# Starting the first pair's scans after the sources of its first image

## The chip, the cores and the metric

The kernel runs on one core of one Trainium2 chip. The metric is device time in microseconds (us); the figure of a kernel is the median of its runs. Five engines work side by side, each with its own queue of instructions in a fixed order: PE (TensorE, matmuls; PEld is its weight loading), DVE (VectorE), ACT (ScalarE), POOL (GpSimd) and SP (SyncE, which here only starts transfers). ACT starts transfers too.

## The reference, cut to what matters

Input and output are 8 images of 64 channels and 64 x 64 pixels, in fp32. Four layers follow each other: an attention over all 4096 pixels with small convolutions (layer 0), two blocks of windowed attention with an MLP (layer 1), a dynamic 3 x 3 filter with a 1 x 9 convolution (layer 2), and a state space layer (layer 3). Only layer 3 concerns the change:

```python
xz = jnp.einsum('bhwc,dc->bhwd', x, in_proj_w) + in_proj_b
xi, z = jnp.split(xz, 2, axis=-1)
xc = jax.nn.silu(_dwconv3(jnp.transpose(xi, (0, 3, 1, 2)), conv_w, conv_b))   # sources of the scans
x_hwwh = [xc, xc transposed over the pixels], each also run backwards          # 4 directions
# per direction k and pixel t, for 128 channels x 16 states:
h = h * jnp.exp(dt_t[..., None] * A) + dt_t[..., None] * B_t[:, :, None, :] * u_t[..., None]
y_t = jnp.einsum('bkcn,bkn->bkc', h, C_t)
y = _ln(y, outnorm_g, outnorm_b) * jax.nn.silu(z)                              # then a last projection
```

Each image has its own scan. What the scan of an image reads (`xc` and its transpose) and what its result is later multiplied with (`silu(z)`) depend on that image alone. This is what the document calls the sources of an image.

## The kernel before, in words

**Pairs of images.** Two images of 64 channels fill the 128 partitions, so the 8 images are 4 pairs. For a pair `p`, `front(p)` (a Python generator) does layers 0 to 2 and then `scan_sources(p)`; `scans(p)` does the scans; `back(p)` does the rest of layer 3.

**The sources.** `scan_sources` first normalises the whole pair into `H3`, 8 chunks of 512 pixels, and stores `X` to memory as `x2`. Then, for each of the two images in turn: 8 matmuls into the bank `pi` (L1610) that ACT copies into a padded picture `XI` (L1613); a 3 x 3 convolution by nine DVE operations for each chunk, the first on L1256 and eight on L1252; a Silu on ACT into `xcv` (L1620), a transposed copy into `XT` (L1621) and a store to `xc` (L1622); four stores of `XT` to `xt` (L1625); and 8 matmuls for `z` with a Silu (L1639) and a store to `zs` (L1640). All these stores are started from ACT's queue. Silu and Exp need different tables on ACT, so a change between them puts an `ACT_TABLE_LOAD` ahead of the operation.

**The scans.** The 2 images x 4 directions x 8 blocks of 512 pixels are 64 units, each of 8 steps, so a pair has 512 steps. A step handles two states: SP fetches rows of B and C, spread to all partitions (L1720); POOL multiplies B by the input (`products`, L1725); ACT makes two exponentials (`dad`, L1747); DVE runs two scans (L1750); ACT keeps the last values (`carry`, L1758); POOL or DVE multiply by C (L1761 and L1765); PE adds the products up (L1789). Once per unit `inputs` loads a block of sources (`xs`, L1697) and makes `du` and the rows of B and C from it. The tiles of B and C have three buffers.

**Work beside the scans.** `scans` takes a generator `beside` with its estimated `cost`. Every `yield` gives a cost in made-up units; after each step the generator is advanced until the work done matches the share of steps done, `cost * (i + 1) / (n - LEAD)` with `n` = 512 and `LEAD` = 24. So the work is spread evenly over 488 steps. Beside the scans of pair 0 runs `front(1)` from layer 1 on; beside pair 1 `back(0)` and `front(2)`; beside pair 2 `back(1)` and `front(3)`; beside pair 3 `back(2)`. The final order on each engine is made by a scheduler that starts from this program order.

**The head.** `begin` runs `front(0)` to its end, with layer 0 of pair 1 beside it (`_Apart.first`, with a pace of its own set by `AHEAD`), and only then opens the buffers of the scans. So before the first scan of image 0 the sources of images 0 and 1 are both made. `front` and `first`, the summed costs of a whole front and of its layer 0, are measured here and set the pace of all later pairs.

Of the kernel before, what the change touches and what calls it, by code (L numbers as in the profile page):

```python
# [19 lines left out]
NCH = L // CH  # L20
WS, NH, HD = 8, 8, 8
SHIFT = 4
TAPS = 9
# [212 lines left out]
class _Net:  # L236
    def __init__(self, ctx, tc, x, packs, layout, out):
        self.tc, self.nc = tc, tc.nc
        self.x, self.out = x, out
        nc = self.nc  # L240
        self.const = ctx.enter_context(tc.tile_pool(name="const", bufs=1))
        self.dram = ctx.enter_context(tc.tile_pool(name="rows", bufs=2, space=bass.MemoryType.DRAM))
        self.packs, self.layout, self.w = packs, layout, {}
        self.load(self.const, (0, 1))
        with tc.tile_pool(name="temp", bufs=1) as temp:
            self.load(temp, (2,))
            self.prepare()
# [410 lines left out]
    def window_attention(self, i, T, pools):  # L658
# [4 lines left out]

        H0, H = self.flat("H0"), self.flat("H")
        H03 = H0.rearrange("p (h w) -> p h w", w=64)
        H5 = H.rearrange("p (y x r c) -> p y x r c", y=8, x=8, c=8)

# [19 lines left out]
        for wy in range(8):  # L687
            cols = slice(wy * CH, (wy + 1) * CH)
            rows = H[:, cols]
            pq = ps.tile([P, CH], F32, name="pq", tag="mm")  # L690
# [10 lines left out]
        def scores(wy, wx):  # L701
# [24 lines left out]
            for half in range(2):  # L726
                nc.tensor.matmul(
                    pv[64 * half : 64 * half + 64],
                    lhsT=H[:, cols],
                    rhs=w[f"vw{i}"],  # L730
# [58 lines left out]
    def mlp(self, i, T, pools):  # L789
        nc, w = self.nc, self.w  # L790
        wk, sm, ps = pools
        H = self.flat("H2")
        self.norm(
            ps, wk, T, w["cen64"], w["avg64"], self.eps[:, 0:1], w[f"norm2_g{i}"], self.norm_to(H, w[f"norm2_b{i}"])
        )
# [362 lines left out]
class _Direct:  # L1158
# [8 lines left out]
    def __init__(self, net, ctx):  # L1167
        self.net, self.tc, self.nc, self.w = net, net.tc, net.nc, net.w
        tc = self.tc
        self.dram = ctx.enter_context(tc.tile_pool(name="mem", bufs=2, space=bass.MemoryType.DRAM))  # L1170
        self.slabs = ctx.enter_context(tc.tile_pool(name="slabs", bufs=3))
        self.ps = ctx.enter_context(tc.tile_pool(name="ps_scan", bufs=3, space=PSUM))
        self.pf = ctx.enter_context(tc.tile_pool(name="ps_front", bufs=3, space=PSUM))
        self.kept = {}
        self.turn = -1
        self.dense = 0

    def begin(self, ctx):


        tc = self.tc
        with tc.tile_pool(name="slabs0", bufs=3) as slabs, tc.tile_pool(name="w00", bufs=2) as pool:
            ahead = _Apart(self, slabs, pool).first(1)
            front = first = done = 0
            for cost in self.front(0):
                front += cost
                if cost == 0:
                    first = front
                while first and done < AHEAD * (front - first):
                    done += next(ahead, front)  # L1190
            self.run(ahead)
        one = ctx.enter_context(tc.tile_pool(name="scan1", bufs=1))
        self.Y = one.tile([P, L], F32, name="Y", tag="Y")
        self.carries = one.tile([P, NST], F32, name="carry", tag="carry")
        self.sw = ctx.enter_context(tc.tile_pool(name="scan", bufs=2))
        return front, first

    def work(self, name):
        return self.tc.tile_pool(name=name, bufs=2)
# [392 lines left out]
    def scan_sources(self, p, X2):  # L1592

        nc, tc, w, net, half = self.nc, self.tc, self.w, self.net, self.HALF
        x2 = self.memory("x2")
        with tc.tile_pool(name="w3", bufs=2) as wk:
            H = self.flat("H3")
            for c in range(NCH):
                cols = slice(c * CH, (c + 1) * CH)
                nc.sync.dma_start(x2[:, cols], X2[:, cols])  # L1600
                pc, sd = self.normed(wk, lambda pc: [(pc, X2[:, cols])], w["cen64"], w["avg64"], net.eps[:, 0:1])
                nc.vector.scalar_tensor_tensor(H[:, cols], pc, w["ln1_g"], sd, ALU.mult, ALU.mult)
                nc.scalar.activation(H[:, cols], H[:, cols], AF.Identity, bias=w["ln1_b"])
                yield 6
            for im in range(2):
                xc, xt, zs = self.memory("xc"), self.memory("xt"), self.memory("zs")
                pad = self.padded("XI")
                for c in range(NCH):
                    pi = self.bank("pi")
                    nc.tensor.matmul(  # L1610
                        pi, lhsT=w["inT"][half[im], 0:P], rhs=H[half[im], c * CH : (c + 1) * CH], start=True, stop=True
                    )
                    nc.scalar.activation(self.rows(pad, c), self.img(pi), AF.Identity, bias=w["in_b"][:, 0:1])  # L1613
                    yield 2
                XT = self.flat("XT").rearrange("p (w h) -> p h w", h=64)
                for c in range(NCH):
                    acc = self.bank("xacc", (P, 8, 64))
                    yield from self.dwconv(acc, pad, 8 * c, 8, w["cw"], w["cb"])
                    cv = wk.tile([P, 8, 64], F32, name="xcv", tag="xcv")
                    nc.scalar.activation(cv, acc, AF.Silu)  # L1620
                    last = nc.scalar.activation(XT[:, 8 * c : 8 * c + 8, :], cv, AF.Copy)  # L1621
                    nc.scalar.dma_start(xc[:, c * CH : (c + 1) * CH], cv.rearrange("p a b -> p (a b)"))  # L1622
                    yield 2
                for s in range(4):
                    nc.scalar.dma_start(  # L1625
                        xt[:, 1024 * s : 1024 * s + 1024],
                        XT.rearrange("p h w -> p w h")[:, 16 * s : 16 * s + 16, :].rearrange("p w h -> p (w h)"),
                    )
                for c in range(NCH):
                    pz = self.bank("pz")  # L1630
                    nc.tensor.matmul(
                        pz,
                        lhsT=w["inT"][half[im], P : 2 * P],
                        rhs=H[half[im], c * CH : (c + 1) * CH],
                        start=True,
                        stop=True,
                    )
                    z = wk.tile([P, CH], F32, name="z", tag="z")
                    last = nc.scalar.activation(z, pz, AF.Silu, bias=w["in_b"][:, 1:2])  # L1639
                    nc.scalar.dma_start(zs[:, c * CH : (c + 1) * CH], z)  # L1640
                    yield 2
                net.log_exp(last)
                self.kept[2 * p + im] = (xc, xt, zs)
        self.kept["x", p] = x2


    @staticmethod
# [264 lines left out]
@with_exitstack  # L1912
def tile_kernel(ctx: ExitStack, tc: tile.TileContext, x: bass.AP, packs, layout, out: bass.AP):
    net = _Net(ctx, tc, x, packs, layout, out)
    with ExitStack() as path:
        net.open(path, True)
        d = _Direct(net, path)
        net.log_exp()
        front, first = d.begin(path)
        back = 0.25 * front  # L1920
        for p in range(B // 2):
            works, cost = [], 0
            if p:
                works.append(d.back(p - 1))
                cost += back
            if p + 1 < B // 2:
                works.append(d.front(p + 1))
                cost += front if p else front - first
            d.scans(p, d.chain(*works), cost)
        d.run(d.back(B // 2 - 1))  # L1930

    with tc.tile_pool(name="check", bufs=1) as pool:
        bad = net.in_range(pool)
    with tc.If(bad > 0), ExitStack() as path:
        net.open(path, False)
        for p in range(B // 2):
            t = net.layer0(p)
            t = net.layer1(t)
            t = net.layer2(t)
            net.layer3(t, p)  # L1940
# [21 lines left out]
```

## Time and profile before

| what | value |
| --- | --- |
| median of 3 runs | 13519.48 us (13518.94, 13519.48, 13551.32) |
| the profiled execution | 13549.57 us, span 13547.6 us |
| busy share of the span: PE, DVE, ACT, POOL | 80%, 65%, 52%, 57% |
| first POOL product of pairs 0, 1, 2, 3 at | 2191.2, 4767.4, 7988.3, 11180.4 us |
| last POOL product | 13279.5 us |
| mean granted TensorE clock | 0.882 |

The times in the trace count from the start of the span. A group's row names line, engine, operation and tiles, then its count, busy time, mean and the idle time of the engine before it with what ended that. "Releaser" is whatever a waiting instruction was waiting for. A row of the stretches gives start and end, length, busy time with instruction count for PE, PEld, DVE, ACT and POOL, then granted clock, the mean busy share of the 16 DMA engines, and GB/s.

### The profile page before, as it was taken

The page shows a single profiled execution, that of the slowest core. Times are in us where ns is not written, and L with a number is a line of the kernel's source. Part 1 is how long each engine was busy: PE and PEld are TensorE (multiplying, and loading weights), DVE is VectorE, ACT ScalarE, POOL GpSimd, SP SyncE. Part 2 cuts the span into 40 slices and gives each one's busy share as a digit, 9 for nine tenths or more (in the row PEclk, how much of TensorE's full clock was granted, in tenths as well). Part 3 has the DMA queues.
Part 4 walks back from the last instruction along what each step waited for, and adds up shares of the span by engine and source line. Part 5 has one row for each costly group of instructions (what it writes and reads, how often), then busy time and mean ns, then how long its engine had stood idle before and what let it go on. Part 6 is the DMA issues. An engine that isn't in the chain of part 4 may idle for free. (4 is left out here: it accounts for less than half of the span.)

```text
span 13547.6 us, 140341 instructions
## 1 busy us (share of the span) xinstructions
PE 10802.4 (80%) x45762; PEld 3981.2 (29%) x45762; DVE 8783.4 (65%) x10407; ACT 7087.6 (52%) x15569; POOL 7764.9 (57%) x3875
## 2 busy tenths in 40 slices
PE   9999986888787669989888667997898666666665
PEld 2243322333232222224432222223443222222221
DVE  0121236776668676676666767667675768988985
ACT  5556514564545646655554545665653644544542
POOL 0000004887778764466666685446675687777881
PEclk9999977998898779999889788998888788888887
DMA  0000004776667765455555674455554677787882
GB/s 24 1 1 1 3 13 170 238 238 211 207 218 244 235 200 168 155 186 175 169 178 175 221 250 168 158 167 176 186 192 151 209 241 262 235 280 264 303 283 86
DMA packets 706249, 2385.12 MB, mean 176 GB/s; under 512 B 81120, under 2 KB 81248, under 8 KB 704480
## 3 DMA queue, kind: packets, MB, share of 16 engines
q1 hardware_dynamic: 681312, 2319.76, 50.9%
q10 hardware_dynamic: 24192, 56.29, 1.1%
q8 instruction: 362, 5.93, 0.2%
q14 instruction: 383, 3.14, 0.1%
HBM read 2272.97 MB, written 102.76 MB: 175 GB/s over the span
## 5 line engine op out<-in xcount | busy, mean ns | idle before, releaser
L1725 POOL TENSOR_TENSOR vd<-B,du 128x1024 f32<-128x1024 f32 x2048 | 4832.8, 2367 | 3924.8 <-DMA B<-rows 2573.0
L1789 PE MATMUL yd<-vd,pack 128*128 128x512 f32 x7540 | 4263.8, 696 | 1381.0 <-POOL vd L1761 591.9
L1747 ACT ACTIVATE dad<-du,As 128x512 f32<-128x512 f32 x4096 | 2729.0, 681 | 1130.8 <-DVE hd L1750 684.1
L1750 DVE TENSOR_TENSOR_SCAN hd<-dad,carry,vd 128x512 f32<-128x512 f32 x2166 | 2713.2, 1270 | 677.8 <-ACT dad L1747 385.9
L1789 PEld LDWEIGHTS yd<-vd,pack 128*128 128x128 f32 x7540 | 1497.0, 215 | 3843.5 <-issue 1654.4
L1761 POOL TENSOR_TENSOR vd<-hd,C 128x1024 f32<-128x1024 f32 x658 | 1551.4, 2358 | 1068.2 <-DVE hd L1750 702.0
L1750 DVE TENSOR_TENSOR_SCAN dad<-dad,carry,vd 128x512 f32<-128x512 f32 x1418 | 1793.3, 1274 | 160.3 <-POOL vd L1725 99.1
L1765 POOL TENSOR_TENSOR vd<-hd,C 128x512 f32<-128x512 f32 x1154 | 1476.1, 1280 | 512.5 <-DVE hd L1750 446.4
L1313 ACT ACTIVATE e<-s 128x512 f32<-128x512 f32 x2048 | 1200.7, 591 | 751.1 <-PE s L1307 749.6
L1307 PE MATMUL s<-X 64*128 64x512 f32 x4096 | 1344.4, 646 | 30.5 <-ACT e L1313 28.8
L1299 PE MATMUL po<-e,VT 128*64 128x512 f32 x4096 | 1226.7, 621 | 12.6 <-ACT e L1313 9.9
L1765 DVE TENSOR_TENSOR vd<-dad,C 128x512 f32<-128x512 f32 x1300 | 864.9, 672 | 48.2 <-ACT carry L1758 39.1
L1758 ACT ACTIVATE carry<-hd 128x1 f32<-128x1 f32 (+1 forms) x1586 | 317.3, 201 | 920.3 <-DVE hd L1750 917.0
L1758 ACT ACTIVATE carry<-dad 128x1 f32<-128x1 f32 x1422 | 240.9, 169 | 804.1 <-DVE dad L1750 801.4
L1307 PEld LDWEIGHTS s<-X 64*128 64x128 f32 x4096 | 375.9, 186 | 915.2 <-issue 783.1
L1447 DVE TENSOR_TENSOR w_e<-w_s,bias 128x512 f32<-128x512 f32 x512 | 329.9, 681 | 424.3 <-PE w_s L1435 423.6
L1462 PEld LDWEIGHTS w_av<-vals,w_e 64*64 64x64 f32 x16384 | 546.7, 144 | 197.3 <-issue 86.8
L1462 PE MATMUL w_av<-vals,w_e 64*64 64x9 f32 x16384 | 574.9, 207 | 30.4 <-ACT w_e L1452 30.1
L1700 PE MATMUL pdd<-xs,xdt 128*128 128x512 f32 x512 | 348.3, 768 | 257.8 <-DMA xs<-xc 121.4
L1452 ACT ACTIVATE w_e<-w_e 128x512 f32<-128x512 f32 x512 | 311.8, 626 | 366.9 <-DVE w_e L1447 251.6
L1299 PEld LDWEIGHTS po<-e,VT 128*64 128x64 f32 x4096 | 236.1, 135 | 847.5 <-issue 763.9
L1574 PE MATMUL acc<-tap,pack 128*128 128x512 f32 x576 | 367.5, 761 | 99.5 <-DVE tap L1573 98.1
(252 smaller groups left out, 11129.2 us busy)
## 6 DMA issues: line engine op xcount, KB each, us to landing
B<-rows SPq DMA_DIRECT2D x2048, 512.0 KB, 5.2
C<-rows SPq DMA_DIRECT2D x2048, 512.0 KB, 4.6
xs<-xt SPq DMA_DIRECT2D x128, 256.0 KB, 3.5
xs<-xc SPq DMA_DIRECT2D x128, 256.0 KB, 4.2
xc<-xcv ACTq DMA_DIRECT2D x64, 256.0 KB, 4.0
zs<-z ACTq DMA_DIRECT2D x64, 256.0 KB, 3.7
xt<-XT ACTq DMA_DIRECT2D x32, 512.0 KB, 7.8
rows<-bc SPq DMA_DIRECT2D x256, 64.0 KB, 1.6
```

The lines of the kernel that those rows point to most:

```text
L1299: nc.tensor.matmul(po[half[im]], lhsT=VT[:, t, half[im]], rhs=es[im], start=(t == 0), stop=(t == 31))
L1307: nc.tensor.matmul(ss[im], lhsT=at(half[im], t), rhs=X[half[im], jc * CH : (jc + 1) * CH], start=True, stop=True)
L1313: nc.scalar.activation(e, ss[im], AF.Exp, scale=C**-0.5, accum_out=parts[:, im, t, jc : jc + 1])
L1462: nc.tensor.matmul(self.av[half[im], x % 4 + j, h, :], lhsT=es[h // 4][half[im], j, h % 4, :], rhs=V[half[im], x + j, h, :], start=True, s ...
L1574: nc.tensor.matmul(acc, lhsT=w["ident"], rhs=tap, start=(t == 0), stop=(t == TAPS - 1))
L1725: self.nc.gpsimd.tensor_tensor(v, st["B"], dx.to_broadcast([P, 2, TD]), ALU.mult)
L1747: nc.scalar.activation(da, u["du"][:, 0], AF.Exp, scale=net.As[:, k, n : n + 1])
L1750: nc.vector.tensor_tensor_scan(along(to), along(da), along(v[:, j]), first, ALU.mult, ALU.add)
L1758: nc.scalar.activation(cs, ends, AF.Copy)
L1761: st["w"] = nc.gpsimd.tensor_tensor(v, h, CC, ALU.mult)
L1765: m = engine.tensor_tensor(v[:, j], hs[j], CC[:, j], ALU.mult)
L1789: m = nc.tensor.matmul(u["y"], lhsT=w["ident"], rhs=v, start=start, stop=stop)
```

## The change

The scans of pair 0 begin once the sources of image 0 exist. `scan_sources` ends each image with `self.ready = 2 * p + im` and a `yield 0`; `begin` stops reading the generator when `ready` is 0, opens the scans' buffers and hands the unfinished generator back. Beside the scans of pair 0 that rest (the sources of image 1) runs first, then `front(1)` as before. Its cost is set to `more` = 8 x (0.7 x 9 + 6) = 98.4 units, which is added to the cost beside pair 0 and to `front`, so that `front` has the same value as before. `H3` is allocated outside the work buffers, and the chunk buffers of each image (`w3i`) are opened and closed for each image, so that none is open while `begin` opens others. The arithmetic is the same.

```diff
@@ class _Direct: __init__, begin
+        self.ready = -1
...
-            for cost in self.front(0):
+            works = self.front(0)
+            for cost in works:
                 front += cost
-                if cost == 0:
+                if cost == 0 and not first:
                     first = front
+                if self.ready == 0:
+                    break
                 while first and done < AHEAD * (front - first):
                     done += next(ahead, front)
             self.run(ahead)
...
-        return front, first
+        return works, front, first
@@ scan_sources
+        H = self.flat("H3")
         with tc.tile_pool(name="w3", bufs=2) as wk:
-            H = self.flat("H3")
...
-            for im in range(2):
+        self.kept["x", p] = x2
+        for im in range(2):
+            with tc.tile_pool(name="w3i", bufs=2) as wk:
                 xc, xt, zs = self.memory("xc"), self.memory("xt"), self.memory("zs")
...
                 self.kept[2 * p + im] = (xc, xt, zs)
-        self.kept["x", p] = x2
+            self.ready = 2 * p + im
+            yield 0
@@ tile_kernel
-        front, first = d.begin(path)
+        rest, front, first = d.begin(path)
+
+        more = NCH * (0.7 * TAPS + 6)
+        front += more
         back = 0.25 * front
         for p in range(B // 2):
-            works, cost = [], 0
+            works, cost = [rest], more
             if p:
+                works, cost = [], 0
                 works.append(d.back(p - 1))
                 cost += back
```

## The prediction

> **What bounds the kernel now.** I read the page first. Its chain of work that ended last covers only a few per cent of the span, nearly all in the closing `back(3)`, so it says nothing of the head. The change lives between the end of layer 2 of pair 0 and the end of pair 0's scans (2191 to 4767 us), so I took the timeline around the first scan (start, duration, engine, operation, and in brackets the idle time before it):
>
> ```profile
> 2098.09 1.70 ACTq L1640 DMA_DIRECT2D zs<-z  x2
> ...
> 2108.09 0.81 DVE L1256 TENSOR_SCALAR xacc<-XI,pack 128x512 f32<-128x512 f32 x1 [22.06 <-ACT XI L1613]
> ...
> 2110.52 10.62 DVE L1252 SCALAR_TENSOR_TENSOR xacc<-XI,pack,xacc 128x512 f32<-128x512 f32 x16
> ...
> 2173.36 1.76 ACTq L1640 DMA_DIRECT2D zs<-z  x2
> ...
> 2177.62 0.80 SPq L1697 DMA_DIRECT2D xs<-xt  x2
> ...
> 2182.75 0.66 ACT L1702 ACTIVATE pdd<-pdd,pack 128x512 f32<-128x512 f32 x1 [2.19 <-PE pdd L1700]
> ...
> 2191.20 4.67 POOL L1725 TENSOR_TENSOR vd<-B,du 128x1024 f32<-128x1024 f32 x2 [2174.44 <-DMA B<-rows]
> ```
>
> The first `zs` row ends image 0's sources, the second image 1's; between them everything is image 1's. POOL has waited 2174 us for its first product. Next the stretches (columns: PE, PEld, DVE, ACT, POOL busy, clock, DMA share, GB/s):
>
> ```profile
> 2085.00:2165.00 80.00, 35.56 (x39) 10.68 (x38) 49.16 (x77) 27.98 (x37) 0.00 (x0) 0.50 0.28 107
> 2787.00:2935.00 148.00, 115.66 (x286) 40.14 (x290) 100.31 (x104) 102.62 (x189) 128.68 (x64) 0.90 0.67 231
> 3589.00:4165.00 576.00, 479.70 (x1011) 173.63 (x1010) 394.12 (x425) 231.47 (x483) 449.36 (x219) 0.90 0.64 213
> 4249.00:4615.00 366.00, 229.42 (x363) 77.19 (x364) 294.47 (x343) 240.36 (x389) 288.67 (x141) 0.79 0.74 246
> ```
>
> Row one is image 1's sources alone in the head: no engine is full. Row two is scans beside an MLP: POOL 87% busy, DVE 68%. The last is scans beside the sources of pair 1, the very work that is moved: DVE rises to 80%, POOL falls to 79%. The groups on the page give the pace that POOL allows:
>
> ```profile
> L1725 POOL TENSOR_TENSOR vd<-B,du 128x1024 f32<-128x1024 f32 x2048 | 4832.8, 2367 | 3924.8 <-DMA B<-rows 2573.0
> L1761 POOL TENSOR_TENSOR vd<-hd,C 128x1024 f32<-128x1024 f32 x658 | 1551.4, 2358 | 1068.2 <-DVE hd L1750 702.0
> L1765 POOL TENSOR_TENSOR vd<-hd,C 128x512 f32<-128x512 f32 x1154 | 1476.1, 1280 | 512.5 <-DVE hd L1750 446.4
> ```
>
> Two steps of pair 0 take POOL 2 x 2.367 + 2.358 + 1.280 = 8.37 us, or 4.19 us a step. The 512 steps took 2576 us, 5.03 each. So pair 0's scans are paced by POOL's work plus 0.84 us a step of waits.
>
> **What the Trainium skill says.** "Perfetto Trace Analysis", section Optimization Strategy, says that a kernel with several regimes can gain from interleaving them; rows one and two above are such regimes (POOL idle, then 87% busy). "ScalarE: Activation LUTs", section What ACT_TABLE_LOAD costs, gives 1283 ns for a load and about 2.66 us for each change of set with its drain. The trace agrees on the load (1283 ns, in every such row) and shows no separate drain: a load at 4613.11 is followed by its Silu at 4614.40. "DMA: Bandwidth & Descriptors", section Issuing engines are not separate DMA queues, says that transfers started on ACT and SP share 16 engines. That fits the share of 0.74 in the sources row against 0.67 beside the MLP.
>
> **The change part by part.**
>
> *Removed from the head.* Today the first `xs` leaves at 2177.62, 2.5 us after the last `zs` of image 1 was started (2173.36 + 1.76 = 2175.12), since it waits for all earlier stores. After the change it waits for image 0's last `zs`, which ends its start at 2098.09 + 1.70 = 2099.79; so it leaves near 2102.3, 75.3 us earlier. The compiled order puts a table load and six of image 1's `XI` copies ahead of the first `pdd` exponential on ACT. In the trace these run from 2099.81, and the sixth, at 2107.37 plus 0.69, ends at 2108.1. The `xs` landing (some 3 us) and two matmuls end at about 2107.5, so ACT decides: `pdd` at 2108.1 instead of 2182.75, 74.7 us earlier. From there the chain to the first product (8.45 us) is unchanged. Gain: 75 us.
>
> *Moved into the scans.* Image 1's sources: DVE 8 x (0.805 + 8 x 0.745) = 54 us of convolution plus 0.4 of border; ACT 8 x (0.69 + 0.60 + 1.08 + 0.69) = 24 us; PE 16 matmuls of some 0.69 us beside scans, 11 us (0.85 in the head, where the clock is 0.50); 20 stores on ACT's queue. Their pace is 1412.8 units over 488 steps, 2.895 a step, so 98.4 units take 34 steps; `front(1)` then has 454 steps instead of 488 and is 7.5% denser.
>
> *Added.* The compiled orders differ in number by 33 table loads, all on ACT: 33 x 1.283 = 42 us, each between scan exponentials. Every other instruction count is the same, and from the end of pair 0 on the orders agree, so pairs 1 to 3 cost the same. ACT is in order, so behind a load wait the next `dad` exponential and `carry`, then DVE's scan, POOL's product with C, and SP's next fetch, which waits for a buffer of B or C.
>
> *Moved on SP.* The load of pair 1's `X` from `first` (2 MB) is ahead of the first `xs` today; it goes in among B and C fetches near step 30. The compiled order gives it no wait but an earlier transfer, so SP isn't blocked; its bytes are those of two steps' fetches. Unloaded it lands in 8.8 us at most: 0 to 9 us, I take 5.
>
> *What the scans pay.* The trace has the same work beside the same scans: 366 us (last row) hold 72 products, 5.08 us a step, and at 1314.4 / 488 = 2.69 units a step an image takes 36.5 steps, so this is two images. Upper comparison: POOL's floor of 4.19, giving 36.5 x 0.89 = 32 us. Lower: the MLP row, 148 us for 32 steps or 4.62, giving 36.5 x 0.46 = 17 us. The last 48 steps of pairs 1 and 2, with little beside them, take 5.0 to 5.1, so steps without other work don't reach the floor; I take 17. Table loads and stalls on stores are in these steps. If all the denser work must be paid in DVE time, the price is 54 us plus most of the 5; if idle time of DVE and ACT covers it, nothing.
>
> Sum: -75 + 17 + 5 = -53. The profiled execution's 13549.6 us would become 13496.6. The median stands 30.1 us below that execution, and I carry the difference over: 13519.5 - 53 = 13466.5, say 13467, 0.39% faster. About 0.3% (41 us) is what a measurement of this kernel can tell from no change.
>
> **The rivals.**
>
> *All hidden.* POOL and the fetches pace pair 0 whatever stands beside it. For: POOL 87% busy beside light work; in the DVE-heavy stretch it still does 79%. Against: it fell by 8 points there. Time: 13519.5 - 75 = 13444.
>
> *DVE becomes the bound.* Scans need 2 x 1.27 + 0.5 x 0.67 = 2.9 us of DVE a step plus about 0.2 of unit work; 54 us over the 23 steps of the convolution add 2.35, in all 5.4, above POOL's 4.19. Then the moved DVE time is paid nearly in full, 57 us with the 5: 13519.5 - 75 + 57 = 13501, within 0.3%. Against: the same overload in the last row came out at 5.08 over both images, as the scheduler spreads the taps.
>
> *Slower: table changes on ACT's queue.* Image 1 has 16 Silus. If each stops the scan chain for two loads, its own 0.69 and a wait for its staging tile, like
>
> ```profile
> 4629.22 1.28 ACT L1639 ACT_TABLE_LOAD   x1 [4.50 <-DMA zs<-z]
> ...
> 4631.31 1.28 ACT L1747 ACT_TABLE_LOAD   x1
> ```
>
> (the store of `z` is late, and the exponentials stand behind it), that is 2.57 + 0.69 + 4.5 = 7.7 us, times 16 is 124 us: 13519.5 - 75 + 124 = 13568, slower by 0.36%. It decides from 4.7 us a Silu (no gain left), 7.2 us for 0.3%. Against: those two images had 32 Silus and cost at most 65 us above POOL's floor, 2 us each.
>
> *It doesn't do what it says.* The scheduler could pull image 1's work ahead of the scans. The compiled order shows only the six copies and ten convolution taps (7.5 us of DVE, while B is on its way) before the first scan, so this is out.
>
> **How the numbers follow.** Likeliest, 0.52: -53, with its own range 13455 to 13479. All hidden 0.13: 13444 to 13455. DVE bound 0.24: 13480 to 13520. ACT 0.09: above 13560. A rest of 0.02 is spread. Faster by over 0.3%: 0.52 + 0.13 = 0.65; within: 0.26; slower: 0.09. The range from 13440 to 13515 leaves out the ACT case and the edge of the DVE case, with little below.
>
> **What would show it.** Right: the first POOL product near 2116; 33 more table loads; pair 0's scans longer by 10 to 35 us, the length of pairs 1 to 3 unchanged within some 15 us (pairs 1 and 2 differ by 29 today). Wrong: the first product later than 2125 (another wait ahead of `xs`); pair 0 longer by over 50 us, with DVE full in the first 40 steps (DVE rival) or ACT waiting for `zs` and `xc` stores (ACT rival); or pair 0 no longer at all. What would break the sum is the denser `front(1)` costing more than in proportion, seen as steps beside layer 2 above today's 5.2.

## The result and the profile after

| kernel, same runs side by side | median us | lowest to highest |
| --- | --- | --- |
| before | 13530.14 | 13518.94 to 13551.32 (5 runs) |
| changed | 13461.74 | 13452.38 to 13465.75 (5 runs) |

The ratio is 0.995, with a 95% interval of 0.9937 to 0.9963: 0.50% faster. The forecast was faster, 13467 us, range 13440 to 13515. The profiled execution of the changed kernel took 13452.38 us, span 13450.6 (before: 13549.57 and 13547.6).

The code has seven more lines ahead of the scans, so L1697, L1702, L1725, L1747, L1750, L1761 and L1765 of before are L1704, L1709, L1732, L1754, L1757, L1768 and L1772 here. First the timeline around the first scan, in the same columns as before:

```profile
2084.49 1.28 ACT L438 ACT_TABLE_LOAD   x1 [1.20 <-issue]
...
2087.21 0.80 SPq L1704 DMA_DIRECT2D xs<-xt  x2
...
2092.05 0.69 ACT L1619 ACTIVATE XI<-pi,pack 128x512 f32<-128x512 f32 x1 [1.02 <-PE pi L1616]
...
2094.05 0.66 ACT L1709 ACTIVATE pdd<-pdd,pack 128x512 f32<-128x512 f32 x1 [1.32 <-PE pdd L1707]
...
2098.26 5.36 DVE L1256 SCALAR_TENSOR_TENSOR xacc<-XI,pack,xacc 128x512 f32<-128x512 f32 x8
...
2102.42 4.64 POOL L1732 TENSOR_TENSOR vd<-B,du 128x1024 f32<-128x1024 f32 x2 [2085.97 <-DVE xacc L1256]
```

`xs` leaves at 2087.21, `pdd` follows at 2094.05, POOL starts at 2102.42. The convolution taps of image 1 (L1256) already stand beside the first exponentials. From the start of image 0's last `z` store (2083.33 here, 2098.66 in the kernel before) to the first product it is now 19.1 us, and it was 92.5.

The stretches (PE, PEld, DVE, ACT, POOL busy with counts, clock, DMA share, GB/s). First the changed kernel's first 40 steps of scans, now beside image 1's sources; then the first 40 steps of the kernel before, beside layer 1 of pair 1:

```profile
2102.00:2303.00 201.00, 121.44 (x193) 40.19 (x194) 153.99 (x175) 134.64 (x223) 160.47 (x79) 0.79 0.76 256
```

```profile
2191.00:2376.00 185.00, 146.25 (x933) 65.19 (x932) 131.25 (x149) 105.26 (x220) 160.18 (x79) 0.90 0.69 230
```

POOL does the same 160 us of work in both; the 16 us that the changed kernel needs more are POOL standing still. No engine is full: POOL is at 80%, DVE at 77%, ACT at 67%. The clock granted to TensorE is lower here, 0.79 against 0.90. The groups of the changed kernel:

```profile
L1732 POOL TENSOR_TENSOR vd<-B,du 128x1024 f32<-128x1024 f32 x2048 | 4830.1, 2366 | 3847.0 <-DVE xacc L1256 2086.3
L1768 POOL TENSOR_TENSOR vd<-hd,C 128x1024 f32<-128x1024 f32 x658 | 1549.6, 2355 | 1057.4 <-DVE hd L1757 740.8
```

Counts and durations are those of before. What moved is POOL's idle time ahead of the products, 3924.8 to 3847.0.

**Where the time went.** The first products of pairs 0 to 3, the last product and the span's end give lengths. The two single executions compare like this:

| stretch | before | changed | difference |
| --- | --- | --- | --- |
| up to image 0's last `z` store (instructions in the same order) | 2098.7 | 2083.3 | -15.3 |
| from there to the first product | 92.5 | 19.1 | -73.4 |
| pair 0's scans | 2576.2 | 2596.8 | +20.6 |
| pairs 1, 2, 3 | 3220.9, 3192.1, 2099.1 | 3202.9, 3187.7, 2095.5 | -18.0, -4.4, -3.6 |
| after the last product | 268.1 | 265.3 | -2.8 |

The first row isn't the change. Up to there both kernels run the same instructions in the same order; about half of it arose before 113 us and the rest between 680 and 800, in stretches where the granted clock of TensorE differed between the two executions (0.81 against 0.94 between 30 and 60 us, 0.76 against 0.83 between 740 and 780). Two later executions of the changed kernel have their first product at 2124.8 and 2122.9, not 2102.4.

For pair 0 I cut its 512 steps into parts and read each part in every execution, since the same kernel repeats a part better than a whole pair. "Without" are the kernel before and one that leaves image 1's sources out (first experiment); "with" are three executions of the changed kernel:

| steps | without (2) | with (3) | difference of means |
| --- | --- | --- | --- |
| 0 to 40 | 184.7, 185.7 | 200.4, 198.4, 201.8 | +15.0 |
| 40 to 96 | 260.9, 262.9 | 261.5, 257.5, 259.1 | -2.5 |
| 96 to 288 | 951.8, 948.3 | 944.8, 950.6, 935.7 | -6.3 |
| 288 to 416 | 660.1, 656.9 | 653.6, 654.0, 649.8 | -6.0 |
| 416 to 464 | 229.0, 232.4 | 240.9, 241.0, 240.8 | +10.2 |
| 464 to 512 | 289.6, 286.7 | 295.6, 287.8, 288.0 | +2.3 |

So the head gives 73.4 us, and the scans take back 15 where image 1's sources stand and 10 where the sources of pair 1 stand. Both differences are three times the spread within their rows or more. All parts together are +12.6 in the means (2587.1 against 2574.6); that sum is less sure, since pair 0 of the changed kernel alone ranges from 2575.3 to 2596.8. The parts are bounded by step numbers, and image 1's sources stand where layer 1 of pair 1 stood: steps 0 to 40 hold 193 matmuls instead of 931, and steps 96 to 288 hold 5700 instead of 4925. A part therefore shows what a place costs, not what one piece of work costs.

### The profile page after: what moved, and what is told of

Same layout as the page of the kernel before. It is cut to its first block, busy times and chain, and to the rows that moved or that the text cites. A ratio compares the mean times of both kernels' runs of the same rounds, so it can differ in the third digit from the quotient of the medians.

```text
span 13450.6 us, 140381 instructions
## 1 busy us (share of the span) xinstructions
PE 10778.6 (80%) x45762; PEld 3973.8 (30%) x45762; DVE 8785.0 (65%) x10407; ACT 7126.2 (53%) x15602; POOL 7763.5 (58%) x3875
## 5 line engine op out<-in xcount | busy, mean ns | idle before, releaser
L1732 POOL TENSOR_TENSOR vd<-B,du 128x1024 f32<-128x1024 f32 x2048 | 4830.1, 2366 | 3847.0 <-DVE xacc L1256 2086.3
L1796 PE MATMUL yd<-vd,pack 128*128 128x512 f32 x7540 | 4313.5, 703 | 1386.1 <-POOL vd L1768 604.8
L1754 ACT ACTIVATE dad<-du,As 128x512 f32<-128x512 f32 x4096 | 2730.9, 681 | 1115.0 <-DVE hd L1757 669.8
L1757 DVE TENSOR_TENSOR_SCAN hd<-dad,carry,vd 128x512 f32<-128x512 f32 x2166 | 2711.5, 1269 | 679.7 <-ACT dad L1754 406.0
L1768 POOL TENSOR_TENSOR vd<-hd,C 128x1024 f32<-128x1024 f32 x658 | 1549.6, 2355 | 1057.4 <-DVE hd L1757 740.8
L1757 DVE TENSOR_TENSOR_SCAN dad<-dad,carry,vd 128x512 f32<-128x512 f32 x1418 | 1793.0, 1274 | 155.5 <-POOL vd L1732 99.3
L1772 POOL TENSOR_TENSOR vd<-hd,C 128x512 f32<-128x512 f32 x1154 | 1475.7, 1280 | 508.7 <-DVE hd L1757 449.1
L1303 PE MATMUL po<-e,VT 128*64 128x512 f32 x4096 | 1227.9, 622 | 12.6 <-ACT e L1317 9.9
L1772 DVE TENSOR_TENSOR vd<-dad,C 128x512 f32<-128x512 f32 x1300 | 865.3, 672 | 54.1 <-ACT carry L1765 44.9
L1765 ACT ACTIVATE carry<-hd 128x1 f32<-128x1 f32 (+1 forms) x1586 | 316.1, 201 | 901.0 <-DVE hd L1757 898.4
L1765 ACT ACTIVATE carry<-dad 128x1 f32<-128x1 f32 x1422 | 240.8, 169 | 807.8 <-DVE dad L1757 804.7
```

What stands on the lines that cost most here:

```text
L1303: nc.tensor.matmul(po[half[im]], lhsT=VT[:, t, half[im]], rhs=es[im], start=(t == 0), stop=(t == 31))
L1732: self.nc.gpsimd.tensor_tensor(v, st["B"], dx.to_broadcast([P, 2, TD]), ALU.mult)
L1754: nc.scalar.activation(da, u["du"][:, 0], AF.Exp, scale=net.As[:, k, n : n + 1])
L1757: nc.vector.tensor_tensor_scan(along(to), along(da), along(v[:, j]), first, ALU.mult, ALU.add)
L1765: nc.scalar.activation(cs, ends, AF.Copy)
L1768: st["w"] = nc.gpsimd.tensor_tensor(v, h, CC, ALU.mult)
```

## The experiments

Each kernel's times below are beside runs of the kernel before on the same chip. Those medians were 13535.37 us (for the kernels without image 1's sources, with three copies, with one tap and without Silu), 13530.47 (blank units, the changed kernel's second measurement, and the two that move more), 13548.48 (its third, and the first two with spread stores) and 13550.39 (the last). Lengths of pairs and parts come from one execution of each kernel.

### Is the head's gain 75 us, and what does the moved work cost?

Image 1's sources are left out, and its scans read those of image 0. No units are counted for them, so `front(1)` is again spread over 488 steps:

```diff
-            works, cost = [rest], more
+            works, cost = [], 0
+            d.kept[1] = d.kept[0] if p == 0 else d.kept[1]
```

> Left out: the sources of image 1 of the first pair are not made at all; its scans and its last step read those of image 0, so the output for image 1 is another. Everything else is the changed kernel (13462 us, pair 0's scans 2597 us between first products). What this saves against it is the price of the moved work beside the scans; what it saves against the kernel before is the price of the same work in the head. My sum: 17 us beside the scans, so about 13445, pair 0 about 2580; 85 less than before. All hidden: 13462, pair 0 about 2597. DVE bound: 54 us, 13408, pair 0 about 2543.

Measured: 13473.54 us (13453.12 to 13487.89), ratio 0.9955 (0.9941 to 0.9969); pair 0 takes 2572.9 us, the length before; the last `z` store is 17.6 us ahead of the first product. So the head's gain needs nothing but the earlier start. The median alone doesn't show the price of the moved work (it is not even below that of the changed kernel); the parts of pair 0 in the table above do. The waits of the first 40 steps say what the moved work does to the scans (engine, waited for, us in total, times, longest). Without image 1's sources:

```profile
DVE hd L1757 <- ACT dad L1754: 6.9, 3, 4.2
DVE du L1713 <- ACT pdd L1712: 5.7, 3, 2.9
POOL vd L1732 <- DMA B<-rows: 2111.2, 5, 2108.6
```

and in the changed kernel:

```profile
DVE hd L1757 <- ACT dad L1754: 18.7, 8, 4.5
DVE du L1713 <- ACT pdd L1712: 14.1, 2, 11.8
POOL vd L1768 <- DVE hd L1757: 8.9, 6, 3.8
POOL vd L1732 <- DMA B<-rows: 12.0, 6, 5.3
```

DVE now waits for ACT's exponentials 12 us longer, and for `pdd`, where a unit changes, another 8. POOL waits for DVE's scans in turn (0.5 us in the first kernel, where 20.1 us of its waits carry no releaser; 5.7 here). But POOL also waits for rows of B to land: 12.0 us, and 2.6 in the first kernel, where the 2108.6 is the wait ahead of the first product. So the rows show two paths to POOL's 16 us, ACT's queue and late fetches, and don't say how much each is worth.

### Is the price proportional to the work?

Image 1's sources are made three times over (the loop around the whole body, and three times the cost):

```diff
+                for again in range(3 if (p, im) == (0, 1) else 1):
+                    pad = self.padded("XI")
+                    for c in range(NCH):
...
-            works, cost = [rest], more
+            works, cost = [rest], 3 * more
```

> The sources of image 1 of the first pair are made three times over into the same places, and their units are counted three times, so the work beside pair 0 has twice the moved work more. My sum: 2 x 17 = 34 us more than the changed kernel, 13496, pair 0 about 2631. All hidden: 13462. DVE bound: 2 x 54 = 108 more, 13570, pair 0 about 2705. ACT rival (66 more table loads and 32 Silus at 4.7 us and more): 150 or more, above 13610.

Measured: 13622.36 us (13618.27 to 13641.82), ratio 1.0066 (1.0052 to 1.008). Pair 0 takes 2745.3 us, 158 more than the changed kernel's mean: some 79 us for each further copy, where I had priced the first at 17 to 22. Steps 40 to 96 take 335.9 us instead of 259.4 (+76), steps 288 to 416, beside layer 2, 721.0 instead of 652.5 (+68). One place in the first of these, a change of unit on ACT:

```profile
2351.25 1.28 ACT L1710 ACT_TABLE_LOAD   x1
2357.35 2.05 PE L1708 MATMUL pdd<-xs,xdt 128*128 128x512 f32 x2 [5.08 <-DMA xs<-xt]
2359.43 0.66 ACT L1710 ACTIVATE pdd<-pdd,pack 128x512 f32<-128x512 f32 x1 [6.90 <-PE pdd L1708]
2361.18 1.28 ACT L1713 ACT_TABLE_LOAD   x1
2363.56 1.28 ACT L1755 ACT_TABLE_LOAD   x1
2368.18 2.35 POOL L1769 TENSOR_TENSOR vd<-hd,C 128x1024 f32<-128x1024 f32 x1 [13.44 <-DVE hd L1758]
```

`xs` took 7.2 us to land; ACT, in order, stood 6.90 us ahead of `pdd`, then loaded two more tables with unit work between, and POOL stood still for 13.44 us. The further copies bring stalls on stores that the first one doesn't have: the four stores of `XT` of the second and of the third, started in a row, keep ACT's queue for 6.96 us (from 2431.02) and 5.95 us (from 2601.82), and ahead of the borders of the next picture DVE stands 17.05 us, until 2617.62, where a store of `XT` ended last; with one copy it stands 1.84 us at that place. So 79 us is the price of a copy made this way and here, and not of the same work anywhere.

### Does the denser front cost the 68 us?

No sources of image 1, but 295 units of nothing in their place, so that the work of `front(1)` is spread over fewer steps:

```diff
-            works, cost = [rest], more
+            works, cost = [iter([2.0] * 144 + [3 * more - 288.0])], 3 * more
+            d.kept[1] = d.kept[0] if p == 0 else d.kept[1]
```

> Left out: the sources of image 1 of the first pair (its scans read those of image 0). In their place stand 295 units of nothing, as many as the kernel with threefold sources counts, so that about 90 steps run alone and the work for pair 1 is packed into the other 398, 22% denser. If the price beside the scans is proportional to the work, pair 0 stays near 2573 us. If denser work costs more than in proportion, which would be the second part of the 150 us that the threefold sources cost, pair 0 takes about 2630.

Measured: 13485.75 us (13473.31 to 13505.81), ratio 0.9966 (0.9953 to 0.9979); pair 0 2589.7. Steps 288 to 416 take 720.1 us, as with three copies (721.0), and 656.9 without blanks; its layer 2 stands in 76 steps instead of 95. But these steps also hold more: 1722 matmuls instead of 1145, because the MLP ahead of layer 2 now reaches to step 333 instead of 294. Steps 96 to 288, which hold 592 matmuls fewer, take 894.4 instead of 948.3, and the pair is only 17 us longer, not the 57 of my expectation. The first steps were not alone, as I had meant them: the compiled order drew the start of `front(1)` into them (its first score matmul stands at step 13, as without blanks). So the 63 us here, and the 68 with three copies (1835 matmuls in these steps instead of 1178), come with work that has moved across step 288. What the packing of `front(1)` costs is the 17 us of the pair, and these are no larger than the spread of a pair.

### Is it DVE's convolution, or ACT's Silus?

Eight of nine taps of image 1 are left out in one kernel; in the other its Silus are replaced by a copy and by a bias add, so that no table changes:

```diff
+                    if (p, im) == (0, 1):
+                        nc.vector.tensor_scalar(acc, pad[:, 8 * c : 8 * c + 8, 0:64], w["cw"][:, 0:1], w["cb"], ALU.mult, ALU.add)
+                        for t in range(TAPS):
+                            yield 0.7
```

> Left out: eight of the nine taps of the convolution of image 1 of the first pair, so 64 DVE operations (48 us) less beside the scans; pace, Silus, table changes and stores stay. The output of image 1 is another. If DVE time is paid: 48 us less than the changed kernel, 13414. My sum: the scans pay 17 us for all of the moved work, and I put 10 of it on the taps: 13452. All hidden, or the price is ACT's: 13462.

```diff
-                    nc.scalar.activation(cv, acc, AF.Silu)
+                    nc.scalar.activation(cv, acc, AF.Copy if (p, im) == (0, 1) else AF.Silu)
...
-                    last = nc.scalar.activation(z, pz, AF.Silu, bias=w["in_b"][:, 1:2])
+                    last = nc.scalar.activation(z, pz, AF.Identity if (p, im) == (0, 1) else AF.Silu, bias=w["in_b"][:, 1:2])
```

> Left out: the Silu of image 1 of the first pair (a copy, and a sum with the bias, in its place), so that its 16 operations need no change of table and about 33 loads (42 us of ACT) are gone; taps, copies and stores stay. The output of image 1 is another. If the price of the moved work is the table changes: 17 to 20 us less than the changed kernel, 13443. If it is DVE's taps: 13462. My sum: half of 17, 13453.

Measured: one tap 13474.71 us (13439.22 to 13502.7), ratio 0.9954 (0.9937 to 0.9971), pair 0 2587.7; no Silu 13465.79 (13448.53 to 13471.13), ratio 0.9946 (0.9931 to 0.996), pair 0 2578.4. The totals tell nothing apart. The first 40 steps take 196.1 and 195.0 us, against 200.2 with everything and 185.2 with nothing. So leaving out 48 us of DVE work is worth 4 us, and leaving out the Silus' tables (1 load stands in these steps instead of 34) is worth 5; each is one execution, and this part varies by 3.4 us in the changed kernel. Neither is the limit alone: about 10 of the 15 us stay whichever is taken.

The kernel with one tap isn't a clean test of DVE, because its compiled order is another: the stores of `XT` begin at step 14 instead of 28, 22 table loads stand in the first 40 steps instead of 34, and the first 16 steps take 79.2 us instead of 65.1, the next 24 117 instead of 135. A further rival is in both: the clock granted to TensorE in these steps is 0.76 to 0.84 in all kernels with image 1's sources and 0.87 to 0.90 without. No run holds the clock apart.

Without the Silus, DVE's wait for ACT's exponentials is down to 1.3 us, but the one at the change of unit is still there:

```profile
DVE du L1713 <- ACT pdd L1712: 18.2, 2, 15.8
DVE hd L1757 <- ACT dad L1754: 1.3, 2, 1.0
```

### The changed kernel again

> The changed kernel as it is, run beside the next three on one chip. The runs so far leave open whether the moved work costs anything beside the scans: pair 0 took 2597 us with it and 2573 without it in single profiles, but the medians are 13462 with it and 13474 without. If pair 0 shows the price, its length is again 2590 to 2605 us and the median 13460 to 13485. If it is hidden, pair 0 is near 2575.

Measured: 13465.06 us (13430.17 to 13482.99), ratio 0.9947 (0.9933 to 0.9962); first product at 2124.8, pair 0 2589.3. The result holds. A third time, in the last but one set:

> The changed kernel once more, beside the two with spread stores: 13455 to 13470, pair 0's scans 2585 to 2600 us, first 40 steps 197 to 201.

Measured: 13489.64 us (13476.57 to 13510.09) beside 13548.48, ratio 0.9957 (0.994 to 0.9973); first product at 2122.9, pair 0 2575.3, first 40 steps 201.8. Its time and its pair 0 were outside what I had written: a whole pair of one and the same kernel ranges over 21 us, while the first 40 steps stay within 3.4.

### Can more be moved?

In the first kernel image 0's `z` also waits until the scans have begun (16 units more beside them). In the second, image 0's convolution after its first two chunks waits too (66 units more), and image 0's first directions are scanned in the order 0, 1, 3, 2, so that the first units need only these chunks:

```diff
+            if apart:
+                self.ready = 0
+                yield 0
+                with tc.tile_pool(name="w3j", bufs=2) as wk:
+                    yield from zees(wk)
...
+        more = NCH * (0.7 * TAPS + 6) + 2 * NCH
```

> Nothing left out. The eight z of image 0 are made beside the scans too, after the first xs. In the head they hold the last two xcv and the stores of XT back; without them the first product should come 5 to 8 us earlier, against 16 units more beside the scans (3 to 4 us). My theory: 0 to 5 us less than the changed kernel. If the scans hide it all: 8 less.

```diff
+                    yield from conv(wk, range(2, NCH))
+                    yield from zees(wk)
...
+            for nth, k in enumerate((0, 1, 3, 2) if p + im == 0 else (1, 3, 0, 2)):
...
+        more = NCH * (0.7 * TAPS + 6) + 2 * NCH + 6 * (0.7 * TAPS + 2)
```

> Nothing left out. Image 0 begins with the forward direction over rows (order 0, 1, 3, 2 instead of 1, 3, 0, 2), and the scans begin when two of the eight chunks of its convolution are stored; six chunks, the transposed copy and z of image 0 and all of image 1 run beside the scans. The first product should come about 49 us earlier than in the changed kernel; 66 units more beside the scans at 17 to 25 us for 98 units are 11 to 17. Theory of a price in proportion: 32 to 38 us less than the changed kernel, about 13430. If the price grows with the amount, as the threefold sources suggest (74 us for each further 98 units): no gain, 13462 or more.

Measured: 13507.33 us (13456.2 to 13529.83), ratio 0.998 (0.9973 to 0.9987), and 13516.93 (13484.81 to 13544.52), ratio 0.9988 (0.9981 to 0.9995): both slower than the changed kernel. The heads did what was meant: from the end of image 0's first `XI` copy to the first product it is 80.0 and 36.8 us, against 84.6 in the changed kernel of the same set, so 4.6 and 47.8 earlier. (The first products stand at 2108.6 and 2056.4, against 2124.8; the rest of these differences arose ahead of the change.) But pair 0 takes 2631.2 and 2680.7 us, 44 and 94 over the changed kernel's mean, which with these gains gives the slower medians. In the second, the extra time lies in every part between steps 40 and 464: +33 in steps 40 to 96, +27 in 96 to 288, +20 in 288 to 416, +13 in 416 to 464. Most of these steps are beside other work than the moved sources. Denser packing alone doesn't explain it, as far as the blank units show: they pack `front(1)` more than either kernel and cost 17 us. What else does was not tested.

### Is it the burst of stores?

At the change of unit in the changed kernel, ACT's row reads

```profile
2226.51 0.39 ACTq L1631 DMA_DIRECT2D xt<-XT  x1
2230.50 0.17 ACT L1765 ACTIVATE carry<-dad 128x1 f32<-128x1 f32 x1 [4.22 <-DVE dad L1757]
2230.51 1.26 ACTq L1631 DMA_DIRECT2D xt<-XT  x2
2238.89 0.66 ACT L1709 ACTIVATE pdd<-pdd,pack 128x512 f32<-128x512 f32 x1 [8.21 <-DMA xt<-XT]
...
2241.34 1.28 ACT L1712 ACT_TABLE_LOAD   x1
...
2243.23 1.28 ACT L1754 ACT_TABLE_LOAD   x1
```

and the stretch

```profile
2226.00:2239.00 13.00, 7.64 (x12) 2.18 (x11) 2.94 (x4) 0.49 (x3) 4.59 (x3) 0.76 1.01 351
```

The DMA engines are full (1.01), and POOL works for 4.6 of 13 us: three stores of 512 KB are on their way while the next unit's `xs` is fetched. So I spread the four stores of `XT`, one ahead of every second `z` matmul, for image 1 alone (`late = 2 * p + im == 1`) and for images 1 to 7 (`> 0`):

```diff
-                for s in range(4):
-                    nc.scalar.dma_start(
+                if not late:
+                    for s in range(4):
+                        store_xt(s)
                 for c in range(NCH):
+                    if late and c % 2 == 0:
+                        store_xt(c // 2)
                     pz = self.bank("pz")
```

> The changed kernel with the four stores of XT (512 KB each) of image 1 started one ahead of every second z matmul, instead of all four together; all else is the same. In the changed kernel these four stores fall at 2226 to 2232 us; from 2226 to 2239 the 16 DMA engines are full (share 1.01), the next unit's xs takes 7.3 us to land instead of some 3.5, ACT stands 8.2 us ahead of pdd, and POOL works for 4.6 of 13 us. If the burst of stores is what the first 40 steps pay (200.4 and 198.4 us in the changed kernel, 184.7 and 185.7 without image 1's work), they take 188 to 194 here and the pair 8 us less (about 2585). If the table loads and convolution are what they pay, the stall goes elsewhere: 197 to 201 and no change. The median moves by less than 10 us from the changed kernel either way, inside its spread.

Measured: 13472.97 us (13444.3 to 13482.88), ratio 0.9942 (0.9924 to 0.9959), beside the changed kernel's 13489.64 in the same set; the two ranges overlap. Pair 0 takes 2582.2, its first 40 steps 197.7, steps 40 to 96 271.2 instead of 259.4. So for pair 0 the burst is not what is paid: the stall went elsewhere. Nor did spreading empty the DMA engines at this place: with one of the four stores on its way they are still 0.97 full (2240 to 2253), since fetches of B and C start in the gap, and `xs` takes 7.2 us to land, against 7.3. ACT's row of this kernel at the same place:

```profile
2243.19 1.28 ACT L1652 ACT_TABLE_LOAD   x1
2244.49 1.27 ACT L1652 ACTIVATE z<-pz,pack 128x512 f32<-128x512 f32 x2
2245.77 1.28 ACT L1716 ACT_TABLE_LOAD   x1
2250.56 0.66 ACT L1716 ACTIVATE pdd<-pdd,pack 128x512 f32<-128x512 f32 x1 [3.51 <-PE pdd L1714]
```

The wait ahead of `pdd` is 3.51 instead of 8.21 us, but two `z` Silus with their two table loads have moved in. The next exponential starts 13.2 us after the last `carry` ahead of the stall (2256.20 against 2243.01), 14.0 before.

> The same spreading of the XT stores for images 1 to 7, all that are made beside scans. If each burst costs some 8 us where it stands, seven of them are worth up to 50 us: about 13410, pairs 0 to 2 shorter by 8, 16 and 16. If a burst costs only where it meets the change of a unit, as in pair 0, less: 13440 to 13460. If transfers are no limit, no change: 13455 to 13470.

Measured: 13456.16 us (13438.89 to 13467.41), ratio 0.9928 (0.9913 to 0.9943). That is in the range written for a burst that costs only where it meets the change of a unit. All five runs are below all five of the changed kernel in that set. Steps 416 to 464 of pairs 1 and 2 take 291.6 and 291.3 us; they take 302.6 to 309.0 in every kernel above. And once more:

> The kernel with the XT stores of images 1 to 7 spread, once more. If its gain over the changed kernel is real, steps 416 to 464 of pairs 1 and 2 take 288 to 295 us again (302 to 309 in all kernels with the four stores together), and the ratio to the kernel before is 0.9915 to 0.9945. If it was an accident of one call, these steps are back at 302 to 309 and the ratio is 0.9945 or more.

Measured: 13450.65 us (13444.85 to 13451.6), ratio 0.9926 (0.9913 to 0.994); these steps take 290.1 and 297.7, the second just above the 288 to 295 that I had written and below every kernel with the stores together. This version beats both kernels, by 0.73% and by about 0.24% (0.9927 over 0.995). The gain lies in the steps around the second image's stores in pairs 1 and 2. Eight of them (440 to 448 of pair 1) take 69.8 us in the changed kernel and 61.6 here. ACT's row there, first of the changed kernel:

```profile
7542.93 3.91 ACTq L1631 DMA_DIRECT2D xt<-XT  x3
7546.89 0.69 ACT L1645 ACTIVATE z<-pz,pack 128x512 f32<-128x512 f32 x1 [4.34 <-DMA xt<-XT]
7547.59 1.28 ACT L1754 ACT_TABLE_LOAD   x1
```

and of the kernel with all stores spread, run the second time:

```profile
7539.98 0.83 ACTq L1631 DMA_DIRECT2D xt<-XT  x2
7540.91 0.69 ACT L1652 ACTIVATE z<-pz,pack 128x512 f32<-128x512 f32 x1 [0.96 <-PE pz L1644]
7541.61 1.28 ACT L1761 ACT_TABLE_LOAD   x1
```

The row shows the last three of four stores; the first started at 7542.58. Starting four in a row keeps ACT for 4.34 us there, and the exponentials queued behind it; spread, it waits 0.96. Over these 8 steps DVE waits for ACT 24.7 us in the changed kernel and 18.4 here, and POOL for DVE 31.9 and 23.2. The compiled order also has 6 table loads fewer in the whole kernel (397 instead of 403). How much of the gain is theirs stays open. Beside pair 0 spreading doesn't help: steps 0 to 96 take 462.2 to 468.9 us in three executions with spread stores and 455.9 to 461.9 in three of the changed kernel. Spreading only the stores of images 2 to 7 was not tried.

## Why the prediction was right

**The head.** Predicted -74.7, measured -73.4 (19.1 us from image 0's last `z` store to the first product here, 17.6 to 18.9 in the first five kernels of the experiments). The chain behind it was right in all but one link: I had ACT's sixth `XI` copy decide when `pdd` starts. The copy ended at 2092.74 and `pdd` came at 2094.05, released by its matmul. The first product was not near 2116 but at 2102.4, because this execution was 15 us ahead before the change's place; 2124.8 and 2122.9 in the other two lie on the other side.

**The moved work.** Predicted 17 + 5 = 22 us, in the first 36.5 steps. Measured there, the load of `X` included: +15.0. The lower comparison (steps beside an MLP) was thus the right one: the first 40 steps take 4.63 us each without image 1's work, as the 4.62 of the row that I used, and 5.00 with it, just under the 5.08 of the other row. What makes these steps longer I had not derived, only read off, and the experiments leave it open too. The load of `X` was not measured apart.

**The denser front.** I costed it at nothing and named it as what would break the sum. It does cost, at another place than the one named: steps 288 to 416 are no slower (-6), but steps 416 to 464, beside the sources of pair 1, take 10.2 us more. They hold more work than before (226 DVE operations instead of 221, 273 on ACT instead of 251, 273 matmuls instead of 244). That isn't the whole cause: with three copies or with blank units they hold 286 on ACT and 287 matmuls and take 234 us. The parts between give back about as much as this takes, so that the term which I had put at nothing came out near nothing for the whole pair; that was not foreseen.

**The sum.** Predicted -53 in all. Head and pair 0 together: -73.4 + 20.6 = -52.8 for the two profiled executions, and -73.4 + 12.6 = -60.8 with the means of pair 0. That the first agrees to 0.2 us is luck, as pair 0 of the changed kernel ranges over 21 us. The medians differ by 68 us in the first set, 65 in the second and 59 in the third (each to within some 20 us). That 13467 came within 6 us of the measured 13461.74 is luck in part as well: the saving was 15 us larger than the 53 that I had summed, and the median of the kernel before, 13519.48 of three runs, became 13530.14 with two more. Pair 1, which I had expected unchanged within 15 us, is 18.0 shorter in the profiled execution; in the other two of the changed kernel it takes 3196.9 and 3225.6, on both sides of the 3220.9 before, so no change of it is shown.

**The table loads.** 33 more, as predicted (15602 ACT instructions instead of 15569), in the first 40 steps 34 instead of none. Their price as a rival, 7.7 us a Silu, is out: 16 Silus would cost 124 us, and without them the first 40 steps are 5 us shorter. The Trainium skill, "ScalarE: Activation LUTs", section What ACT_TABLE_LOAD costs, gives 2.66 us for a change of set; an estimate from that figure is 16 x 2 x 2.66 = 85 us if nothing hid it. The trace shows each load at 1.28 us with the operation right behind it, and 33 loads at 42 us of ACT; leaving them out made the first 40 steps 5 us shorter.

**DVE as the bound.** Out: DVE is 77% busy in the first 40 steps, and 48 us less of its work, if in another order, saves 4.

**All hidden.** Out where it says that the steps stay as they are: two parts are longer by 15 and 10 us, each three times its spread or more. Not out for the total: neither the medians nor the +12.6 of the pair, with a range of 21 us, exclude a price near nothing.

**Where my reasoning failed.** In the expectations. I took the price as proportional (17 us for 98 units) and so expected little for more work: three copies cost 158 us over one, image 0's `z` 44 us for 16 units, and the later convolution with it 94 us for 66. The first image is cheap where it stands. Six of its copies and ten taps stand before the first scan, and the first 16 steps of the changed kernel take 4.06 us each, as without image 1's work (4.09 and 4.03). The portions behind it cost far more. And I took one cause to be behind the first 40 steps, in turn taps, Silus and stores: each one removed gave 2.5 to 5 of 15 us. They lie behind each other in ACT's queue at the change of a unit, where the fetch of `xs`, the stores and the table loads meet. Taking two of them away at once was not tried, nor were the late rows of B or the lower clock tested, so this is the reading of the rows and not shown by a run.

## What to carry to other kernels

Work that stands alone ahead of a long stage costs its whole length (73.4 us here), and a limited amount of it cost a fifth of that beside the stage; the portions tried next cost more than they saved (44 us against 4.6, 94 against 47.8), so move portion by portion and measure each. Cut the stage into parts whose lengths repeat within a few us, and compare parts, when the total varies by 30 us between executions. A burst of stores on a queue that also feeds a chain can be a cost of its own, at some places and not at others: spreading four stores over eight matmuls, which also saved six table loads, was worth another 0.24%.

## What the runs showed that was not expected

- The same instructions in the same order took 2102.4 to 2124.8 us up to the first product in three executions of the changed kernel. Between the profiled executions of before and after, 15 us arose in the same way, in stretches where the granted clock of TensorE differed (0.81 against 0.94 between 30 and 60 us).
- Scan steps are far steadier. Steps 440 to 448 of pairs 1 and 2 took 69.6 to 72.3 us in twelve executions of ten kernels with the stores of these pairs together, and 61.6 to 64.6 in two executions with them spread.
- A load of 256 KB (`xs`, 122 to 127 us after the first product) that landed in 3.7 and 5.0 us beside layer 1 took 7.3 us while the 16 DMA engines were full (share 1.01, 351 GB/s), and 7.2 with most of the stores gone from that place (0.97, 340 GB/s).
- A change of table showed no time beyond its load of 1.28 us: at 2243.23 a load, at 2244.52 the exponential.
